# Two graph-attention layers on one core: a planner's costs re-read from the profile, the first adjacency load planned later, one attention ranked last

## The chip, the cores and the metric

The kernel runs on one core of a Trainium2 chip. Its time is the device time of one launch in microseconds; a profile of one further execution shows what each engine did. The engines are PE (TensorE, matmuls; "PEld" is its weight load), DVE (VectorE), ACT (ScalarE), POOL (GpSimd) and SP (SyncE, which only issues DMA transfers here).

## The reference

Input: 32 graphs of 512 nodes with 512 features each (`x`), and an integer adjacency matrix of 512 x 512 per graph (`adj`). Two layers, both of the form x = x + GNN(relu(layernorm(x))):

```python
# layer 0
s_src, s_dst = h @ w_src, h @ w_dst
scores = leaky_relu(s_src[:, :, None] + s_dst[:, None, :] + b, 0.2)
attn = softmax(where(adj + eye == 0, -inf, scores), axis=-1)
x = x + attn @ h
# layer 1: two GAT layers; mask = (adj > 0) | eye
xl = (h @ W1).reshape(B, N, 4, 256)          # W2: one head of 512
e = leaky_relu(asrc[:, :, None, :] + adst[:, None, :, :], 0.2)
attn = softmax(where(mask, e, -1e9), axis=1)
out = einsum('bsdh,bshf->bdhf', attn, xl)    # 4 heads side by side
h = elu(out + b1);  then the same with W2, att2, b2 and one head
x = x + h
```

So each graph has six attentions over 512 x 512: one in layer 0, four heads in the first GAT layer (width 256), and one in the second GAT layer (width 512, called the second attention here).

## The kernel before

All is in float32. Nodes lie in T = 4 tiles of 128 partitions. A graph passes through these pieces, each of which only records operations:

- `load_x`, `load_adj`: x of a graph by SP, its adjacency (converted to bf16) by POOL's queue. `load_adj` runs twice per graph, for layer 0's mask (m0) and for layer 1's (m1).
- `layer0_scores`: `layernorm` (DVE statistics, POOL computes the power -1/2 in L516), `relu_normed` on ACT (L529), two dot products per tile on DVE (L384, in `dot`), the mask `masks0` (DVE L758 and L761; then one DMA transpose m0 -> m0T, L735), and `edge_weights`.
- `edge_weights` builds exp(leaky_relu(a_i + c_j) + mask - m_j). A row of scores comes over all partitions, either by four TensorE transposes (`spread`, L506) or by a DMA through DRAM (`in_lines` L605 and L611, `row_of` L621) and a copy into PSUM on ACT (`in_bank`, L631). DVE takes the masked maximum of each tile (L643, with a small accumulator read after it), sums and leaky-relus the maxima (L649, L651), and the result is brought over all partitions by `spread` (L506) or lines. Then, per tile: Prelu on ACT (L665), subtraction of the maximum on DVE (L668), addition of the mask on POOL (L671), exp on ACT (L674).
- `attend` / `aggregate`: matmuls of E with the values (L684), on DVE a reciprocal of the denominator (L696) and the scaled addition to x (L702). `layer1_head` does the same for a head (L970, L973), then the elu (ACT L987, L990 and DVE L994 or, for the last head, L1009 and L1013), and turns the result round: by two ACT copies and a DMA transpose (L558, L565, L574) or by TensorE (L506, for head 3 only).
- `layer1_project`, `layer2_project`: the products with W1 and W2 in a seven-product (Strassen-like) form, L900, with sums of operands on DVE or POOL (`combine`, L881 or L882), results copied (`taken`: L539 on ACT or L545 on DVE) or added (`added`: L913 on DVE).
- `layer2_out`: the second attention of a graph and the store of its output.

What a graph needs twice is put away in DRAM in between (`spill`, `load_back`).

Nothing runs in the order of the calls. Each call of `op` appends an entry: the engines that may do it, a cost per engine, what it reads and writes, and a shift of its rank. A cost is (time it occupies the engine, time until its result is there). `Plan.run` makes six drafts with different weights of the shifts. Each is a list schedule: the engine that is free first takes the ready operation of lowest rank, buffers are given out as they come free, an operation with two engines goes to the one that comes to it first. The draft with the earliest planned end is built, and each engine then runs its list strictly in order, waiting on semaphores. So a cost changes no instruction as such; it changes the order, the engine of operations that have two, and the buffers.

Costs are given by small functions of the number n of elements per partition: `on_dve(n)` is n/0.96 + 70 ns (85 ns more to its end), `on_act(n, i)` is n/1.2 plus one of three constants (i = 0, 1 or 2: none, one or two per-partition operands), and 60 ns more to its end. The main loop at the end goes over the graphs b: `masks1(b)`, `layer1_project(b)`, `load_back(b - 1)`, `layer2_out(b - 1)`, the four heads of b, `layer0_out(b + 1)`, `layer1_in(b + 1)`, `layer0_scores(b + 2)`, `layer2_project(b)`. For the last graph but one, `layer2_out` is split: its first EARLY tiles come in the loop, the rest after the loop, so with the highest ranks but for the last graph's own.

The planner orders by these lines (rank is the place of the call minus a part of the shift `ahead`; a smaller rank goes first):

```python
draft = self.draft([i - part * ahead for i, ahead in (o[5] for o in self.ops)])
...
_, i = heapq.heappop(now[e])
```

Of the kernel before, what the change touches and what calls it, by code (L numbers as in the profile page):

```python
# [241 lines left out]
def on_dve(n, speed=1.0, scaled_psum=False):  # L242
    one = n / 0.96 / speed + (130.0 if scaled_psum else 70.0)
    return one, one + 85.0


def on_act(n, per_partition=0):

    one = n / 1.2 + (95.0, 140.0, 280.0)[per_partition]
    return one, one + 60.0  # L250


def on_pool(n, narrow=False):
# [15 lines left out]
def kernel(  # L269
# [24 lines left out]
    nc = tc.nc  # L294
    B, N, D = x.shape
    H, F = att_src1.shape
# [17 lines left out]
    def node_tiles(src: bass.AP, b: int) -> bass.AP:  # L314
        return src[b].rearrange("(t p) f -> p t f", p=P)
# [124 lines left out]
    def scores_1(att):  # L440
        for k in range(KD):
            for h in range(H):
                q, kk = QUARTER[k // (KD // 2)][h % 2], k % (KD // 2)
                for i in range(2):
                    op(
                        "DVE", on_dve(F),
                        lambda w=w1_s[q][:, kk, h // 2, :], i=i, h=h: dot(
                            w[:, 2:], flat(att[0])[:, i * HF + h * F : i * HF + (h + 1) * F], w[:, i : i + 1]
                        ),
                        W["w1"]((q, kk)) + att[0](i), W["w1"]((q, kk, h // 2, i)), -LATER, lock=True,  # L450
                    )

    def scores_2(att):
        part = const.tile([P, KH, 2], F32, name="part")
        for k in range(KH):
            (q, r), kk = QUARTER[k // (KH // 2)], k % (KH // 2)
            lo, hi = w2_s[q][:, kk, :], w2_s[r][:, kk, :]
            for i in range(2):
                op(
                    "DVE", on_dve(W2),  # L460
                    lambda lo=lo, i=i, k=k: dot(lo[:, 2:], flat(att[1])[:, i * D : i * D + W2 - 2], part[:, k, i : i + 1]),
                    W["w2"]((q, kk)) + att[1](i), W["w2"](("part", k)), -LATER, lock=True,
                )
                op(
                    "DVE", on_dve(W2),
                    lambda lo=lo, hi=hi, i=i: dot(hi, flat(att[1])[:, i * D + W2 - 2 : (i + 1) * D], lo[:, i : i + 1]),
                    W["w2"]((r, kk)) + att[1](i), W["w2"]((q, kk, i)), -LATER, lock=True,
                )
            op(
                "DVE", on_dve(2), lambda lo=lo, k=k: nc.vector.tensor_add(lo[:, :2], lo[:, :2], part[:, k, :]),  # L470
                W["w2"]((q, kk, 0), (q, kk, 1), ("part", k)), W["w2"]((q, kk, "a")), -LATER,
            )
# [62 lines left out]
    def evict(src, dst, src_of, dst_of, n, bias=None, psum_half=False):  # L535

        def by_act():
            if bias is None:
                nc.scalar.copy(dst_of(), src_of())  # L539
            else:  # L540
                nc.scalar.activation(dst_of(), src_of(), AF.Identity, bias=bias)

        def by_dve():
            if bias is None:
                nc.vector.tensor_copy(dst_of(), src_of())  # L545
            else:
                nc.vector.tensor_scalar(dst_of(), src_of(), -1.0, None, op0=ALU.add)

        op(("ACT", "DVE"), (on_act(n, bias is not None), on_dve(n)), (by_act, by_dve), src, dst)

    def turned(values_of, src, place, results_of, dst):

        e = Buffer("row")
        op(
            "ACT", (1040.0, 1100.0),
            lambda: nc.scalar.copy(  # L558
                e.at.bitcast(U16).rearrange("p (b f) -> p b f", b=2), values_of().bitcast(U16).rearrange("p (f b) -> p b f", b=2)
            ),  # L560
            src + place, e(0),
        )
        op(
            "SP", by_turning(4 * P * N),
            lambda: nc.sync.dma_start(  # L565
                values_of().bitcast(U16).rearrange("p (c n) -> p c n", n=P), e.at.bitcast(U16), transpose=True
            ),
            e(0), src,
        )

        def pair():
            out = results_of()
            k, t = out.shape[1], out.shape[2]
            nc.scalar.copy(  # L574
                out.bitcast(U16).rearrange("p k t (n b) -> p k t n b", b=2),
                values_of().bitcast(U16).rearrange("p (b t k n) -> p k t n b", b=2, k=k, t=t),
            )

        op("ACT", (1160.0, 1220.0), pair, src, dst)

    def spread(part, col_of, ahead):

# [51 lines left out]
    def edge_weights(kind, scores, ac, lines, k, mask_max, mask, near):  # L634


        a_of = lambda t: ac.at[:, k, t : t + 1]
        a_row = spread(scores, a_of, AHEAD) if lines is None else in_bank(row_of(lines, k))
        amax, z, m = Buffer("col"), Buffer("col"), Buffer("col")
        for t in range(T):  # L640
            op(
                "DVE", on_dve(N + 60),
                lambda t=t: nc.vector.tensor_tensor_reduce(  # L643
                    by_blocks(junk), mask_row(mask_max, t), by_blocks(a_row.at), 1.0, LOWEST, ALU.add, ALU.max,
                    accum_out=amax.at[:, t : t + 1],
                ),
                a_row(*ROW) + mask_max(*ROW), amax(t),
            )
        op("DVE", on_dve(T), lambda: nc.vector.tensor_add(z.at, ac.at[:, k + 1, :], amax.at), scores + amax(*ROW), z(0))  # L649
        op(  # L650
            "DVE", on_dve(T), lambda: nc.vector.scalar_tensor_tensor(m.at, z.at, SLOPE, z.at, op0=ALU.mult, op1=ALU.max),  # L651
            z(0), m(0),
        )

        E = Buffer(kind)
        m_row = (
            spread(m(0) + E("place"), lambda t: m.at[:, t : t + 1], AHEAD) if near
            else in_bank(row_of(in_lines(lambda: m.at, m(0), 1), 0))
        )
        c_of = lambda t: ac.at[:, k + 1, t : t + 1]  # L660
        c_row = spread(scores + E("place"), c_of, AHEAD) if lines is None else row_of(lines, k + 1)
        for t in range(T):
            op(
                "ACT", on_act(N, 1),
                lambda t=t: nc.scalar.activation(E.at[:, t, :], c_row.at, AF.Prelu, bias=a_of(t), scale=1.0, alpha=SLOPE),  # L665
                c_row(*ROW) + scores, E(t),
            )
            op("DVE", on_dve(N), lambda t=t: nc.vector.tensor_sub(E.at[:, t, :], E.at[:, t, :], m_row.at), m_row(*ROW) + E(t), E(t))  # L668
            op(
                "POOL", on_pool(N, True),  # L670
                lambda t=t: nc.gpsimd.tensor_add(by_blocks(E.at[:, t, :]), by_blocks(E.at[:, t, :]), mask_row(mask, t)),  # L671
                E(t) + mask(*ROW), E(t), lock=True,
            )
            op("ACT", on_act(N), lambda t=t: nc.scalar.activation(E.at[:, t, :], E.at[:, t, :], AF.Exp), E(t), E(t))  # L674
        return E
# [42 lines left out]
    def load_adj(b, m):  # L718

        first, early = not START.wrote, len(adj_loads) < 3
        adj_loads.append(b)
        op(
            "POOL", (1100.0, 5500.0) if first else (2200.0, 16000.0 if early else 8000.0), lambda: nc.gpsimd.dma_start(m.at, node_tiles(adj, b)),  # L725
            () if first else START(0), m(*ROW) + (START(0) if first else []),
        )

# [57 lines left out]
    def layer0_scores(b):  # L786
        rstd, nmr = layernorm(X[b])
        h0, ac = Buffer("h"), Buffer("ac")
        for t in range(T):
            relu_normed(h0, X[b], t, rstd, nmr)  # L790
            for i, w in ((1, ws_r), (0, wd_r)):
                op(
                    "DVE", on_dve(D), lambda t=t, w=w, i=i: dot(h0.at[:, t, :D], w, ac.at[:, i, t : t + 1]),
                    h0(t) + W["w0"](0, 1), ac((i, t)), lock=True,
                )
        c = ac(*((1, t) for t in ROW))
        op(
            "DVE", on_dve(T), lambda: nc.vector.tensor_scalar(ac.at[:, 1, :], ac.at[:, 1, :], b0_r, None, op0=ALU.add),
            c + W["w0"](2), c,
        )  # L800
        m0, m0T = masks0(b)
        scores = c + ac(*((0, t) for t in ROW))

        L0[b] = (h0, edge_weights("E_one", scores, ac, in_lines(first(ac, 2), scores, 2) if b else None, 0, m0, m0T, not b))
# [266 lines left out]

    EARLY = 1
    load_x(0)
    att = load_constants()
    layer0_scores(0)
# [61 lines left out]
```

## Time and profile before

| | us |
|---|---|
| median of 3 runs | 3646.97 (3645.85 to 3647.93) |
| the profiled execution | 3648.51 |
| its span, first to last instruction | 3646.7 |
| PE busy, matmuls | 3542.6 (97%) |
| DVE busy | 2851.2 (78%) |
| ACT busy | 2264.6 (62%) |
| POOL busy | 1424.6 (39%) |
| mean granted TensorE clock | 0.994 |

The profile's groups name a line, an engine and an operation with its tiles, then count, busy time and mean duration. "Idle before, releaser" is the time its engine stood idle just before, and what ended that. The biggest groups:

```
L684 PE MATMUL acc<-pair,E 128*128 128x257 f32 x4096 | 920.4, 379 | 2.4 <-ACT row L987 2.4
L643 DVE CUSTOM_DVE_ANT_0 junk<-m1T,acc 128x512 bf16<-128x512 bf16 x640 | 436.6, 682 | 11.4 <-PE acc L506 3.4
L674 ACT ACTIVATE E<-E 128x512 f32<-128x512 f32 x512 | 315.6, 623 | 161.7 <-POOL E L671 161.4
L671 POOL TENSOR_TENSOR E<-E,m 128x512 f32<-128x512 f32 x512 | 605.1, 1211 | 455.3 <-DVE E L668 396.7
```

Two records stand for one float32 matmul, and matmuls overlap: the records of one are 0.217 us apart, though each shows 0.38.

### The profile page before, as it was taken

What the parts mean: (1) busy time and instruction counts of PE and PEld (TensorE: products, weight loads), DVE (VectorE), ACT (ScalarE), POOL (GpSimd) and SP (SyncE); (2) the same over time, 40 slices, a digit from 0 to 9 for tenths busy, and PEclk for the clock granted to TensorE, in tenths of its full rate; (3) what the DMA queues carried; (4) which work ended last, traced back from release to release, by engine and by line L of the source; (5) the groups of instructions that cost most, each with busy time, mean ns of one, the idle gap of its engine ahead of it and who ended that gap; (6) DMA issues with size and microseconds to landing.
All of it is one profiled execution on the core that took longest, in us unless ns stands there. A gap on an engine that the chain in (4) does not pass through costs nothing.

```text
span 3646.7 us, 50543 instructions
## 1 busy us (share of the span) xinstructions
PE 3542.6 (97%) x16852; PEld 3036.1 (83%) x16852; DVE 2851.2 (78%) x7367; ACT 2264.6 (62%) x3929; POOL 1424.6 (39%) x1279
## 2 busy tenths in 40 slices
PE   4899999999999999999999999999999999999998
PEld 3788888888888888888888888888888888888887
DVE  7978778877778877778787788877787877887755
ACT  2666566665666665666666667655666656666554
POOL 4534334434334343334343344343343433343422
PEclk9999999999999999999999999999999999999999
DMA  6244433444433444334443334443334443344321
GB/s 172 77 105 119 104 92 104 100 121 113 96 96 103 104 121 112 90 96 105 115 116 98 95 103 99 125 116 86 97 110 105 119 108 89 103 103 118 105 73 41
DMA packets 510374, 378.82 MB, mean 104 GB/s; under 512 B 348344, under 2 KB 386976, under 8 KB 510112
## 3 DMA queue, kind: packets, MB, share of 16 engines
q1 hardware_dynamic: 476320, 342.03, 32.8%
q0 software_dynamic: 33792, 33.56, 6.1%
q8 instruction: 132, 2.16, 0.2%
q14 instruction: 130, 1.06, 0.1%
HBM read 257.16 MB, written 68.01 MB: 89 GB/s over the span
## 4 chain that ended last, share of the span: by engine, by line
PE 80%; DVE 14%; ACT 2%; issue 1%; DMA 1%; POOL 0%; DVEq 0%; ACTq 0%; SPq 0%
PE acc L684 45%; PE acc L900 32%; DVE junk L384 5%; PE acc L506 3%; DVE v L1013 1%; DVE hT L881 1%; DVE hT L545 1%; DVE col L521 1%; DVE col L649 1%; ACT h L529 1%; DVE v L973 1%; PE acc L605 1%; DVE junk L643 1%; DVE E L881 1%; DVE xl L913 1%
## 5 line engine op out<-in xcount | busy, mean ns | idle before, releaser
L684 PE MATMUL acc<-pair,E 128*128 128x257 f32 x4096 | 920.4, 379 | 2.4 <-ACT row L987 2.4
L684 PEld LDWEIGHTS acc<-pair,E 128*128 128x128 f32 x4096 | 771.7, 189 | 115.5 <-ACT row L987 2.8
L671 POOL TENSOR_TENSOR E<-E,m 128x512 f32<-128x512 f32 x512 | 605.1, 1211 | 455.3 <-DVE E L668 396.7
L900 PE MATMUL acc<-w_T,E 128*128 128x257 f32 (+1 forms) x2048 | 517.9, 380 | 0.8 <-POOL w_T L488 0.8
L684 PE MATMUL acc<-h,E_one 128*128 128x256 f32 (+1 forms) x2048 | 491.2, 381 | 8.6 <-ACT E_one L674 7.5
L684 PE MATMUL acc<-xl,E_one 128*128 128x257 f32 x1984 | 447.9, 381 | 2.7 <-ACT E_one L674 2.7
L643 DVE CUSTOM_DVE_ANT_0 junk<-m1T,acc 128x512 bf16<-128x512 bf16 x640 | 436.6, 682 | 11.4 <-PE acc L506 3.4
L900 PEld LDWEIGHTS acc<-w_T,E 128*128 128x128 f32 x2048 | 385.4, 189 | 61.0 <-POOL w_T L488 1.5
L684 PEld LDWEIGHTS acc<-h,E_one 128*128 128x128 f32 x2048 | 380.8, 191 | 63.6 <-ACT E_one L674 8.3
L684 PEld LDWEIGHTS acc<-xl,E_one 128*128 128x128 f32 x1984 | 371.8, 190 | 54.7 <-ACT E_one L674 3.1
L674 ACT ACTIVATE E<-E 128x512 f32<-128x512 f32 x512 | 315.6, 623 | 161.7 <-POOL E L671 161.4
L913 DVE TENSOR_TENSOR pair<-acc,pair 128x258 f32<-128x258 f32 (+1 forms) x390 | 165.4, 426 | 293.7 <-PE acc L900 219.2
L539 ACT COPY pair<-acc 128x258 f32<-128x258 f32 (+1 forms) x456 | 165.8, 370 | 320.5 <-PE acc L900 315.8
L665 ACT ACTIVATE E<-row,ac 128x512 f32<-128x512 f32 x512 | 341.1, 707 | 2.4 <-DMA row<-lines 2.4
L668 DVE TENSOR_TENSOR E<-E,acc 128x512 f32<-128x512 f32 x512 | 330.4, 678 | 6.5 <-PE acc L506 3.1
L671 POOL TENSOR_TENSOR E_one<-E_one,m0T 128x512 f32<-128x512 f32 x128 | 144.4, 1152 | 355.6 <-DVE E_one L668 355.6
L725 POOL DMA_DIRECT2D m<-in_adj_dram x64 | 51.5, 805 | 590.8 <-DVE col L643 540.7
L900 PE MATMUL acc<-w,hT 128*128 128x258 f32 x1024 | 265.5, 384 | 0.6 <-issue 0.5
L900 PE MATMUL acc<-w,E 128*128 128x257 f32 (+1 forms) x1024 | 264.2, 380 | 0.0
L702 DVE SCALAR_TENSOR_TENSOR x<-acc,r,x 128x256 f32<-128x256 f32 x512 | 239.7, 479 | 30.9 <-PE acc L684 22.8
L529 ACT ACTIVATE h<-x,col,col 128x512 f32<-128x512 f32 x256 | 187.6, 804 | 109.0 <-DVE col L521 109.0
L539 ACT COPY xl<-acc 128x257 f32<-128x257 f32 x218 | 77.6, 369 | 284.9 <-PE acc L900 284.8
(113 smaller groups left out, 6171.9 us busy)
## 6 DMA issues: line engine op xcount, KB each, us to landing
row<-lines SPq DMA_DIRECT2D x442, 256.0 KB, 3.4
x<-in_x_dram SPq DMA_DIRECT2D x32, 1024.0 KB
m<-in_adj_dram POOLq DMA_DIRECT2D x64, 512.0 KB, 6.3
spill<-x SPq DMA_DIRECT2D x32, 1024.0 KB, 4.2
x<-spill SPq DMA_DIRECT2D x32, 1024.0 KB
out_dram<-x SPq DMA_DIRECT2D x30, 1024.0 KB, 4.2
v<-row SPq DMA_TRANSPOSE x192, 2.7
out_dram<-x SPq DMA_DIRECT2D x8, 256.0 KB, 2.0
```

What stands on the lines that cost most here:

```text
L384: nc.vector.scalar_tensor_tensor(junk[:, : vector.shape[1]], values, 1.0, vector, op0=ALU.mult, op1=ALU.mult, accum_out=out)
L529: lambda: nc.scalar.activation(h.at[:, t, :D], X.at[:, t, :], AF.Relu, bias=nmr.at[:, t : t + 1], scale=rstd.at[:, t : t + 1]),
L539: nc.scalar.copy(dst_of(), src_of())
L643: lambda t=t: nc.vector.tensor_tensor_reduce(by_blocks(junk), mask_row(mask_max, t), by_blocks(a_row.at), 1.0, LOWEST, ALU.add, ALU.max, a ...
L665: lambda t=t: nc.scalar.activation(E.at[:, t, :], c_row.at, AF.Prelu, bias=a_of(t), scale=1.0, alpha=SLOPE),
L668: op("DVE", on_dve(N), lambda t=t: nc.vector.tensor_sub(E.at[:, t, :], E.at[:, t, :], m_row.at), m_row(*ROW) + E(t), E(t))
L671: lambda t=t: nc.gpsimd.tensor_add(by_blocks(E.at[:, t, :]), by_blocks(E.at[:, t, :]), mask_row(mask, t)),
L674: op("ACT", on_act(N), lambda t=t: nc.scalar.activation(E.at[:, t, :], E.at[:, t, :], AF.Exp), E(t), E(t))
L684: lambda s=s: nc.tensor.matmul(acc.at[:, :n], E.at[:, s, node_block(t)], of(s), start=(s == 0), stop=(s == T - 1)),
L702: lambda acc=acc, r=r, f=f, t=t: nc.vector.scalar_tensor_tensor(X.at[:, t, f], acc.at[:, :HD], r.at, X.at[:, t, f], op0=ALU.mult, op1=ALU. ...
L900: lambda k=k: nc.tensor.matmul(acc.at[:, :width], at[a]()[:, k, node_block(r)], weight_of(w, k, c), start=(first and k == 0), stop=(k == n ...
L913: op("DVE", on_dve(width), lambda: nc.vector.tensor_add(place(), acc.at[:, :width], place()), acc(0) + token, token)
```

## The change

Most lines change the planner's costs. Only one thing is different in what the calls record: EARLY is 0, so all four tiles of graph 30's second attention are recorded after the loop.

```diff
 def on_act(n, per_partition=0):
-    one = n / 1.2 + (95.0, 140.0, 280.0)[per_partition]
-    return one, one + 60.0
+    one = n / 1.2 + (95.0, 186.0, 280.0)[per_partition]
+    return one, one + 130.0
+
+def on_act_copied(n):
+    one = n / 1.2 + 52.0
+    return one, one + 160.0
...
# scores_1: dot products with the attention vectors of the first GAT layer
-                        "DVE", on_dve(F),
+                        "DVE", on_dve(F + 125),
...
# scores_2, twice
-                    "DVE", on_dve(W2),
+                    "DVE", on_dve(W2 + 125),
...
# evict
-        op(("ACT", "DVE"), (on_act(n, bias is not None), on_dve(n)), (by_act, by_dve), src, dst)
+        op(("ACT", "DVE"), (on_act_copied(n) if bias is None else on_act(n), on_dve(n)), (by_act, by_dve), src, dst)
...
# turned
-            "ACT", (1040.0, 1100.0),
+            "ACT", (945.0, 1100.0),
...
-        op("ACT", (1160.0, 1220.0), pair, src, dst)
+        op("ACT", (1062.0, 1220.0), pair, src, dst)
...
# edge_weights, the masked maximum
-                "DVE", on_dve(N + 60),
+                "DVE", on_dve(N + 10),
...
# load_adj
-            "POOL", (1100.0, 5500.0) if first else (2200.0, 16000.0 if early else 8000.0), ...
+            "POOL", (1100.0, 11000.0) if first else (2200.0, 16000.0 if early else 8000.0), ...
...
# layer0_scores
-                    "DVE", on_dve(D), lambda t=t, w=w, i=i: dot(...),
+                    "DVE", on_dve(D + 125), lambda t=t, w=w, i=i: dot(...),
...
-    EARLY = 1
+    EARLY = 0
```

More of the change, by code (lines that the diff above doesn't have):

```diff
@@ L464, in scores_2 @@
                 op(
-                    "DVE", on_dve(W2),
+                    "DVE", on_dve(W2 + 125),
                     lambda lo=lo, hi=hi, i=i: dot(hi, flat(att[1])[:, i * D + W2 - 2 : (i + 1) * D], lo[:, i : i + 1]),
@@ L724, in load_adj @@
         op(
-            "POOL", (1100.0, 5500.0) if first else (2200.0, 16000.0 if early else 8000.0), lambda: nc.gpsimd.dma_start(m.at, node_tiles(adj, b)),
+            "POOL", (1100.0, 11000.0) if first else (2200.0, 16000.0 if early else 8000.0), lambda: nc.gpsimd.dma_start(m.at, node_tiles(adj, b)),
             () if first else START(0), m(*ROW) + (START(0) if first else []),
@@ L792, in layer0_scores @@
                 op(
-                    "DVE", on_dve(D), lambda t=t, w=w, i=i: dot(h0.at[:, t, :D], w, ac.at[:, i, t : t + 1]),
+                    "DVE", on_dve(D + 125), lambda t=t, w=w, i=i: dot(h0.at[:, t, :D], w, ac.at[:, i, t : t + 1]),
                     h0(t) + W["w0"](0, 1), ac((i, t)), lock=True,
```

## The prediction, made before the changed kernel was run

> **What bounds the kernel now.** I read the windows view first, for how much TensorE idles and where.
>
> ```profile
> core 0: us, PE busy (x) PEld busy (x) DVE busy (x) ACT busy (x) POOL busy (x), PEclk, DMA share, GB/s
> 0.00:100.00 100.00, 51.54 (x203) 40.30 (x203) 79.02 (x241) 25.94 (x48) 46.01 (x44) 0.91 0.64 168
> 100.00:200.00 100.00, 89.93 (x405) 74.76 (x406) 84.68 (x221) 61.02 (x102) 43.79 (x38) 0.95 0.25 71
> 200.00:2000.00 1800.00, 1784.14 (x8540) 1532.91 (x8539) 1426.32 (x3674) 1150.63 (x2005) 709.79 (x638) 1.00 0.40 106
> 3500.00:3647.00 147.00, 130.40 (x585) 110.08 (x583) 73.12 (x180) 64.64 (x116) 36.06 (x31) 0.94 0.22 63
> ```
>
> The first 200 us hold 58.5 us of TensorE idle (48.46 + 10.07), the last 147 hold 16.6, and the middle 15.9 in 1800. The chain of waits repeats every 110.81 us in the middle, one period per graph, so the middle loses about 1 us per graph. No matmul is added or dropped by this change, so only these gaps can move. The wait view, cut to 1000 to 3216 us (20 periods), says what the middle gaps are:
>
> ```profile
> PE acc L506 <- DVE col L651: 11.7, 20, 0.7
> PE acc L506 <- DVE v L1013: 4.8, 20, 0.2
> ```
>
> Per period that is 0.58 us for one broadcast of a head's row maximum (L506 after DVE's L651), and 0.24 us for one transpose of head 3's result. Around the first of them DVE has no gap:
>
> ```profile
> 2003.39 0.16 DVE L651 SCALAR_TENSOR_TENSOR col<-col 128x4 f32<-128x4 f32 x1
> 2003.51 0.69 DVE L643 CUSTOM_DVE_ANT_0 junk<-m1T,acc 128x512 bf16<-128x512 bf16 x1
> ...
> 2009.46 1.06 DVE L649 TENSOR_TENSOR col<-ac,col 128x4 f32<-128x4 f32 x1
> 2010.45 0.68 DVE L643 CUSTOM_DVE_ANT_0 junk<-m1T,acc 128x512 bf16<-128x512 bf16 x1
> ...
> 2011.45 0.14 DVE L651 SCALAR_TENSOR_TENSOR col<-col 128x4 f32<-128x4 f32 x1
> ```
>
> The reader is to see a stretch where DVE, not TensorE, paces the work: between two maxima 8.06 us pass on DVE (2003.39 to 2011.45), while TensorE has 7.1 us of work between the two broadcasts. The start is a chain of its own; TensorE's timeline:
>
> ```profile
> 33.59 15.88 PE L684 MATMUL acc<-h,E_one 128*128 128x257 f32 x64 [3.42 <-ACT E_one L674]
> 55.51 3.68 PE L506 MATMUL acc<-ident,h 128*128 128x128 f32 x16 [6.04 <-ACT h L529]
> 73.17 0.38 PE L605 MATMUL acc<-ident,ac 128*8 128x128 f32 x1 [9.30 <-DVE ac L798]
> ```
>
> **What the Trainium skill says.** "GPSIMD Engine Reference", Specifications, gives GpSimd an SBUF interface shared with VectorE, with contention for DVE instructions with two SBUF inputs. The trace agrees: the L649 above, four elements wide with both inputs in SBUF, took 1.06 us where the same operation took 0.15 at 2002.71, and it ended with one of POOL's four 1.13 us mask additions (2006.00 to 2010.50). The planner knows nothing of this for L649. "DMA: Bandwidth & Descriptors", Queues, rings and completion order, says that each DMA engine takes its ring's descriptors in order. The first mask's transpose (DMA into m0T) fits it: eight weight loads were still outstanding at its issue, and it landed 9.9 us later.
>
> **The change part by part.** The edits alter planned costs only; so I compare the changed program's order of instructions with the trace.
>
> *Costs.* Some come nearer to the trace: four Prelus (L665) take 2.56 us, 0.62 apart (planned 0.567, now 0.613), two copies of 258 columns stand 0.26 apart (planned 0.310, now 0.267), the interleaving copies 0.95 and 1.06. One goes away from it: four masked maxima (L643) with their accumulator reads take 2.80 us (2101.23 to 2104.03); the plan had 4 x 0.666 = 2.66 and now has 2.46. So in the DVE-paced stretch the new plan is 0.34 us per head too hopeful, before 0.14. Over the program 88 evictions of 258 columns move from ACT to DVE (three per graph, 0.34 us each), 52 additions of 512 columns from DVE to POOL, 27 of 2x256 back. These lie in the projections, where DVE waits for TensorE anyway (gaps of 0.4 to 4 us in that timeline), so I price them at nothing; with that cover gone they would be about 1 us per graph.
>
> *The middle.* TensorE's order repeats every 286 matmuls in both programs. A matmul pair of records is 0.435 us. I go broadcast by broadcast.
> - First: a copy of the last projection result now stands on DVE ahead of the second attention's subtractions. TensorE finishes that product 0.43 us later than before, at 2099.5 of this trace's time; then come 0.2 latency, 0.34 + 0.2 copies, 2.4 subtractions, 2.8 maxima, 0.7 small ones: L651 at 2106.15, broadcast possible at 2106.35. TensorE is there at 2105.26 + 2 x 0.435 = 2106.13. Stall 0.2, before none.
> - Second: DVE gets one more L702 (0.40), TensorE one more matmul (0.435). No stall.
> - Third: TensorE has 13 matmuls since the second broadcast, before 15: 6.2 us. DVE drops one L970 and one L973 (0.5 us) and keeps the rest: 8.06 - 0.5 = 7.57, if L649 again runs into POOL's additions, which start 0.76 us after the first subtraction in both. The spare 0.39 us that before had at the second broadcast is gone. Stall 7.57 - 6.2 = 1.37, before 0.58. With no port wait it would be 0.5.
> - Fourth: 18 matmuls in place of 20 (8.35 us with the broadcast); DVE has one L994 and one L973 fewer, one mask conversion more: 8.9 - 0.5 = 8.4. Stall 0.1.
> - Head 3's transpose: nine matmuls stand ahead of it in place of six, 1.3 us more than needed. Its 0.24 goes.
> Sum 0.2 + 0 + 1.37 + 0.1 = 1.7 against 0.82: +0.87 us per graph. The order repeats for 28 graphs: +24 us. Bounds: every such stall gone, -0.82 x 28 = -23; all port waits at their longest (1.1 us at two more places), half the time, +1.9 x 28 = +53. I take +24, because each term is a count of rows with a duration, and the same count gives before's 0.58 back (8.06 + 0.2 - 7.1 - 0.6 of slack).
>
> *The start.* The mask is expected later (11 us, before 5.5), so SP's queue now holds the transpose into m0T behind all of the second layer's weights and graph 1's x, nine loads further down. These are 3.7 MB; DMA is busy to 45 us in the trace at some 270 GB/s. The second mask load of that pile is issued later, so the pile ends at 42 to 43. m0T then lands there, not at 27.3. And POOL's queue has graph 1's rstd (L516), which needs that x and DVE's four statistics (3.1 us), ahead of the first four mask additions: these begin at about 46 in place of 31.73. Queued behind them is everything: ACT's exps, the first attention, DVE's x. So the first attention starts near 48 and the first product near 73, where before had 59.2. What is won back: after 16 records of products before's TensorE waited 9.30 us for graph 1's scores (L798), and lesser stalls of 2.1 followed; the new order has 26 matmuls ahead of that transpose, 11 us, and the scores are ready. All 112 product records take 24.4 us, so they end near 99; the first head then waits for its rows, to about 109, where before began it at 114.3 but had done half of graph 1's attention (7 us) too. Sum +2 us. Earlier things (ACT's first h at 10.8, before 16.36) gain nothing, since the mask gates. Bounds: m0T early after all, -8; nothing won back, +14.
>
> *The end.* EARLY = 0 ranks graph 30's whole second attention last. Yet TensorE takes whatever is ready: in the new order its 32 matmuls again all stand before graph 31's last projection (3, 7, 11 and 11 among the heads; before 4, 8, 11, 7 and 2). None is left for the waits of 3.00 and 2.74 us before the last attention. The two that stood between the last two head transposes are gone, where before still waited 1.18: +0.5, bounds -1 and +2.
>
> Sum: span 3646.7 + 24 + 2 + 0.5 = 3673. The profiled execution took 3648.5, 1.8 above its span and 1.5 above the median of the runs; so 3673.5, and I say 3673.
>
> **The rivals.**
> - *Paced as before.* The port waits fall elsewhere, DVE's spare time absorbs its copies, and the start is even: within 7 us. For it: the two orders differ by two or three matmuls per stretch only. Against: DVE has no gap there. About 3648.
> - *The better costs win (faster).* ACT's latency, planned at 60 ns before and 130 now, was what made the broadcasts late, and the 9.3 us at the start come without the late mask: 3647 - 23 - 9 = 3615. For it: nearly all edits are nearer to the trace. Against: in 20 periods ACT caused TensorE only two waits, 1.9 us.
> - *The late mask alone (slower).* The middle stays, the start loses its 14 us because later work has the same chain to wait for: 3661. It decides once m0T lands after 40.
> - *EARLY does not do what it says*: held by the order itself, and part of my forecast.
>
> **How the numbers follow.** Forecast 0.55, of which nearly all is slower; paced as before 0.18; faster 0.15; late mask alone 0.12. A change under 0.2% (7.3 us) can't be told from none here. Faster: 0.15. Same: 0.18 less its tails plus 0.02 of the forecast's low end, 0.17. Slower: 0.68. The forecast's own range is 3655 to 3695; the range for 8 in 10 goes down to 3640 to hold the paced-as-before case.
>
> **What would show it.** In the middle: the period above 111.3 us, DVE's L651 as releaser of TensorE's L506 with 1.2 to 2 us per graph in place of 0.58, and no wait on L1013. At the start: m0T landing after 40, the first attention at 46 to 50, no 9 us wait on L798. At the end: 64 records of xl,E_one before the last projection. A period of 110.8 or less refutes the middle step; a first attention before 38 refutes the step on the mask.

## The result, and the profile after

| | before | after |
|---|---|---|
| median, 20 runs each | 3646.84 us (3645.11 to 3650.36) | 3653.77 us (3650.93 to 3661.58) |
| the profiled execution | 3648.51 | 3652.49 |
| its span | 3646.7 | 3650.7 |

The ratio is 1.0018, 95% interval 1.0012 to 1.0025: 0.18% slower, 6.9 us. It lies just inside the 0.2% that I had called no change, and 19 us under the forecast. The profiled executions are only 4.0 us apart: before's was 1.7 above its median, after's 1.3 below.

The windows view of the changed kernel, the same stretches as shown of before (busy us of each engine with its count, the granted clock, DMA):

```profile
0.00:100.00 100.00, 48.13 (x202) 39.45 (x202) 80.17 (x228) 25.57 (x47) 38.74 (x39) 0.97 0.58 161
100.00:200.00 100.00, 86.22 (x387) 70.84 (x388) 86.26 (x223) 59.54 (x99) 45.80 (x40) 0.91 0.30 74
200.00:2000.00 1800.00, 1784.54 (x8526) 1527.50 (x8525) 1406.98 (x3700) 1139.35 (x1954) 731.35 (x648) 1.00 0.41 105
3500.00:3647.00 147.00, 133.56 (x614) 112.30 (x613) 75.86 (x184) 68.79 (x122) 40.98 (x35) 0.97 0.21 62
```

TensorE does 7.1 us less in the first 200 us (3.4 + 3.7), and the same in the middle: 1784.5 against 1784.1. The wait view of 1000 to 3216 us says why the middle is even:

```profile
PE acc L511 <- DVE col L656: 15.2, 20, 0.8
PE acc L689 <- ACT E_one L679: 2.6, 3, 1.6
```

(L511, L654, L656 of the changed kernel are L506, L649, L651 of before: lines past 253 stand five further down.) TensorE spreads a row of maxima over the partitions four times per graph. The third of these broadcasts waits 0.76 us per graph in place of 0.58; the 0.24 before head 3's transposes are gone. 0.76 against 0.82: nothing.

To split the span I follow one record that comes twice per graph, TensorE's transposition of four maxima into a line (L605 before, L610 after). The third of its 62 is at 204.3 us before and 208.7 after, the 61st at 3420.4 and 3425.3. So the start gives +4.4 us, the 29 periods between +0.5, and the end -0.9 (226.3 and 225.4 us to the last instruction). Most periods are 110.82 before and 110.74 after; the others are longer, by 5 us in all after and by 2 before, which takes back what the common period gains. TensorE's timeline of the start:

```profile
46.30 15.91 PE L689 MATMUL acc<-h,E_one 128*128 128x257 f32 x64 [13.02 <-ACT E_one L679]
72.68 6.48 PE L905 MATMUL acc<-w,hT 128*128 128x258 f32 x26
101.66 2.09 PE L905 MATMUL acc<-w_-T,hT 128*128 128x258 f32 x4 [3.83 <-DVE pair L918]
109.37 1.11 PE L511 MATMUL acc<-ident,col 128*128 128x128 f32 x4 [3.22 <-DVE col L656]
113.23 2.08 PE L689 MATMUL acc<-pair,E 128*128 128x257 f32 x4 [2.75 <-ACT E L679]
```

The first attention starts 12.7 us later than before (33.59), the first product 13.5 later; after that the 9.3 us wait for graph 1's scores is gone, and the three waits shown from 101.66 on, together 9.8 us, and one of 1.8 us at L610 stand ahead of the first head. What the first mask additions waited for is seen on GpSimd:

```profile
43.26 1.20 POOL L521 TENSOR_TENSOR col<-col,minus_half 128x4 f32<-128x4 f32 x1 [5.70 <-DVE col L519]
44.44 3.56 POOL L676 TENSOR_TENSOR E_one<-E_one,m0T 128x512 f32<-128x512 f32 x3
```

By the DMA's semaphore the mask m0T had landed at 39.7 us, just behind graph 1's x at 37.9. The additions then stood 4.7 us longer in GpSimd's queue, behind L521, which waited for VectorE's statistics of that x.

### The profile page after: what moved, and what is told of

It reads as the page before. It is cut to its first block, busy times and chain, and to the rows that moved or that the text cites. A ratio compares the mean times of both kernels' runs of the same rounds, so it can differ in the third digit from the quotient of the medians.

```text
span 3650.7 us, 50258 instructions
## 1 busy us (share of the span) xinstructions
PE 3542.4 (97%) x16852; PEld 3027.7 (83%) x16852; DVE 2827.3 (77%) x7427; ACT 2249.2 (62%) x3844; POOL 1471.7 (40%) x1304
## 4 chain that ended last, share of the span: by engine, by line
PE 75%; DVE 20%; issue 1%; DMA 1%; ACT 0%; POOL 0%; SPq 0%; DVEq 0%; ACTq 0%
PE acc L905 41%; PE acc L689 30%; DVE junk L648 7%; DVE E L673 4%; DVE x L707 4%; PE acc L511 4%; DVE E_one L673 2%; DVE col L654 1%; PE acc L610 0%; DVE r L701 0%; DVE v L978 0%; DVE pair L550 0%; DVE col L656 0%; DMA lines<-row 0%; DMA row<-lines 0%
## 5 line engine op out<-in xcount | busy, mean ns | idle before, releaser
L676 POOL TENSOR_TENSOR E<-E,m 128x512 f32<-128x512 f32 x512 | 594.5, 1192 | 408.2 <-DVE E L673 272.0
L689 PE MATMUL acc<-h,E_one 128*128 128x257 f32 (+1 forms) x2048 | 479.9, 380 | 16.7 <-ACT E_one L679 15.7
L648 DVE CUSTOM_DVE_ANT_0 junk<-m1T,acc 128x512 bf16<-128x512 bf16 x640 | 436.0, 681 | 13.8 <-PE acc L511 3.4
L544 ACT COPY pair<-acc 128x258 f32<-128x258 f32 (+1 forms) x368 | 137.9, 375 | 304.0 <-PE acc L905 299.6
L730 POOL DMA_DIRECT2D m<-in_adj_dram x64 | 51.6, 806 | 577.1 <-DVE col L648 527.6
L676 POOL TENSOR_TENSOR E_one<-E_one,m0T 128x512 f32<-128x512 f32 x128 | 144.7, 1154 | 331.6 <-DVE E_one L673 331.6
L905 PE MATMUL acc<-w,E 128*128 128x257 f32 (+1 forms) x1024 | 271.8, 380 | 0.0
L707 DVE SCALAR_TENSOR_TENSOR x<-acc,r,x 128x256 f32<-128x256 f32 x512 | 238.8, 477 | 28.3 <-PE acc L689 26.0
L905 PE MATMUL acc<-w,pair 128*128 128x257 f32 x1024 | 253.5, 380 | 0.0
```

The source lines that it names most:

```text
L648: lambda t=t: nc.vector.tensor_tensor_reduce(by_blocks(junk), mask_row(mask_max, t), by_blocks(a_row.at), 1.0, LOWEST, ALU.add, ALU.max, a ...
L689: lambda s=s: nc.tensor.matmul(acc.at[:, :n], E.at[:, s, node_block(t)], of(s), start=(s == 0), stop=(s == T - 1)),
L707: lambda acc=acc, r=r, f=f, t=t: nc.vector.scalar_tensor_tensor(X.at[:, t, f], acc.at[:, :HD], r.at, X.at[:, t, f], op0=ALU.mult, op1=ALU. ...
L905: lambda k=k: nc.tensor.matmul(acc.at[:, :width], at[a]()[:, k, node_block(r)], weight_of(w, k, c), start=(first and k == 0), stop=(k == n ...
```

## The experiments

Medians of 4 to 21 runs; the kernel before, beside them, had 3646.7 to 3648.6, so a difference of 2 us between two rows of the table says nothing. "Period" is the commonest distance of the marker above in one profiled execution, "start" its third record.

| run | edits on before, or the kernel it starts from | us | start | period |
|---|---|---|---|---|
| changed kernel | all | 3653.77 | 208.7 | 110.74 |
| e1 | changed, first mask at 5.5 us | 3653.76 | 203.7 | 110.74 |
| e2 | changed, EARLY = 1 | 3653.15 | 208.2 | 110.75 |
| e3 | changed, maxima at N + 60 | 3643.12 | 217.5 | 110.29 |
| e16 | changed without these three edits | 3636.61 | 207.4 | 110.29 |
| e6 | changed, attention really kept | 3660.50 | 207.7 | 110.76 |
| e5 | changed, half of L707 | 3645.03 | 208.8 | 110.47 |
| e9 | changed, L654 planned at 950 | 3635.45 | 213.8 | 110.13 |
| e10 | changed, maxima at N + 92 | 3661.46 | 204.6 | 110.5 to 113.5 |
| e13 | changed, L654 from PSUM | 3653.09 | 210.2 | 110.75 |
| e17 | changed, L654 and L656 from PSUM | 3629.81 | 209.4 | 109.91 |
| e4 | on_act_copied alone | 3624.65 | 205.1 | 110.02 |
| e7 | e4, half the attention kept | 3627.36 | 205.9 | 110.02 |
| e8 | on_act_copied, on_act | 3631.37 | 204.7 | 110.08 |
| e11 | on_act_copied, L654 at 950 | 3648.11 | 207.7 | 110.75 |
| e12 | on_act_copied, turned | 3616.10 | 202.5 | 109.75 |
| e14 | e12, L654 from PSUM | 3619.42 | 206.6 | 109.75 |
| e15 | e12, first mask at 11 us | 3615.86 | 203.6 | 109.75 |
| e18 | e15, L654 and L656 from PSUM | 3615.21 | 203.9 | 109.75 |

### Which edit moved the time: e1, e2, e3, e16

```diff
# e1                          # each starts from the changed kernel
-   (1100.0, 11000.0) if first
+   (1100.0, 5500.0) if first
# e2
-    EARLY = 0
+    EARLY = 1
# e3
-   "DVE", on_dve(N + 10),
+   "DVE", on_dve(N + 60),
# e16: all three
```

> The changed kernel with the first adjacency load planned at 5.5 us again. All engines run the same order as the changed kernel from about the fourth graph on; only the start differs. Theory A (the start pays for the late mask): the changed kernel is 4.4 us behind at the end of its first graph, its middle takes the same as before and its end 0.9 less; so with m0T landing near 27 and the first attention near 34, nearly all of the difference goes: about 3648 to 3650, 4 to 6 us less than the changed kernel. Theory B (my forecast's start, the late mask costs only about 2 because later waits are won back): 2 us less, about 3652. Theory C (the difference is in the middle): no change, 3653 to 3654. Period 110.74 in all three.

> The changed kernel with EARLY = 1 again. Start and middle have the same order on every engine; only the last 280 of 9173 TensorE instructions differ: three matmuls of graph 30's second attention stand between the last two head transposes, none in the changed kernel. My forecast's end term: 0.5 us less than the changed kernel (range 2 less to 1 more). Rival: the whole attention does fill waits at the end, and undoing it costs 3 us or more.

> The changed kernel with the masked maximum planned at N + 60 again (0.666 us; the trace shows 0.70 for each). In the repeating part TensorE then has 15 matmuls between the second and third broadcast of row maxima, 13 in the changed kernel, and VectorE nearly the same rows in that stretch (8.8 against 8.7 us by the mean durations). Theory A (the cost that went away from the trace makes the third broadcast late): its wait of 0.77 us per graph falls by up to 0.8, the period from 110.74 to 110.0 to 110.2, 15 to 20 us in 28 graphs: about 3635. Theory B (the lateness only moves to another broadcast or transpose): period 110.7 to 110.9, within 3 us of the changed kernel.

> The changed kernel without three of its edits: maxima at N + 60, first mask at 5.5, EARLY = 1. What is left are the costs that come nearer to the trace. Its repeating part has the matmul counts of the run with the maxima at N + 60 (period 110.28, a wait of 0.47 for the first weights of layer 0). Theory A: period 110.28 and a start near 205 in place of 217, so about 3631. Theory B (its start is the one with late first graphs): 3640 to 3645.

e1: theory A had the start right (203.7, five us earlier) and the time wrong: no gain came of it (3653.76 and 3653.77). With the early mask the order of the first graphs is another one, and the four periods after the third record take 111.6, 111.5, 112.0 and 111.9 us: 4.1 us more than four of 110.74. So the five us are given back at once. Even its start has a longer wait for graph 1's scores than before:

```profile
PE acc L610 <- DVE ac L803: 13.0, 1, 13.0
```

e2: 0.6 us under the changed kernel, with ranges that overlap: EARLY as such does nothing that can be told. e3: the lowered maxima cost 10.6 us. The third broadcast's wait is gone, but only half of it is gained, since the next one in line comes up, the first weights of layer 0's attention, 0.47 us per graph:

```profile
PE acc L689 <- ACT E_one L679: 9.5, 20, 0.5
```

e16 has that period too, and a start ten us earlier than e3's; the A expectations of the two were 8 and 6 us too low. The two edits that e16 takes back beyond e3's, mask and EARLY, are worth 6.5 us here, though each alone gave nothing on the changed kernel (e1, e2): what an edit is worth depends on the order that the others make. The costs that came nearer to the trace make the kernel 0.3% faster (ratio 0.9968, 0.9955 to 0.9980); the other three edits take that away and more.

### The attention really kept for the end: e6, e7

```diff
# the matmuls of graph 30's kept tiles also wait for the last projection result of graph 31
-                E(s) + values(*part(s)) + result("place"), acc(0),
+                E(s) + values(*part(s)) + result("place") + list(after), acc(0),
...
-    layer2_out(B - 2, ROW[EARLY:], False)
+    layer2_out(B - 2, ROW[EARLY:], False, L2[B - 1][1]((1, T - 1)))
# e6 on the changed kernel; e7 on e4, with EARLY = 2
```

> The changed kernel, with graph 30's second attention really kept: its matmuls also wait for the last graph's last projection result. Only the last 220 TensorE instructions differ: all 32 matmuls (13.9 us) stand behind the last projection, none between the last graph's heads. Theory A (they are worth what they fill): the waits of 0.7, 3.0 and 2.8 us before the last attention go, but 13.9 us of work stand there, and the heads they left become VectorE's; 2 to 6 us slower than the changed kernel. Theory B (the end was short of work, the heads not): 4 to 6 us faster.

> The kernel of the copies alone (3624.65), with the last two tiles of graph 30's second attention kept behind the last projection (EARLY = 2 and the same wait). Only the end differs. 16 matmuls, 6.9 us, against waits of 6.4 us there, and 6.9 us less work among the last graph's heads. Theory A: 1 to 4 us faster, about 3622. Theory B (the heads then wait for VectorE as long as they ran before): even or slower, 3625 to 3630.

6.7 and 2.7 us slower than the kernels they start from (e7's runs overlap with e4's at the edge). In e6's wait view from 3500 us on, the waits before the last attention are gone and larger ones stand among the heads:

```profile
PE acc L511 <- DVE col L656: 9.3, 2, 4.9
PE acc L511 <- DVE v L1018: 3.9, 2, 2.4
PE acc L689 <- ACT E L679: 2.8, 1, 2.8
```

13.9 us of matmuls found only some 6.5 us of waits to fill; where they had stood, VectorE's maxima are late. All of e6's loss lies there: from the 61st record to the last instruction it takes 232.1 us, the changed kernel 225.4. So the edit gains nothing where it does nothing (the changed kernel, where all 32 matmuls ran ahead of the last projection), and loses where it does what its words say.

### What the third broadcast waits for: e5, e9, e10, e13, e17

The changed kernel's VectorE, from the second broadcast's row (L656 at 2122.22) to the third's:

```profile
2122.22 0.15 DVE L656 SCALAR_TENSOR_TENSOR col<-col 128x4 f32<-128x4 f32 x1
...
2127.59 0.16 DVE L975 RECIPROCAL r<-acc 128x1 f32<-128x1 f32 x1
2127.67 0.92 DVE L654 TENSOR_TENSOR col<-ac,col 128x4 f32<-128x4 f32 x1
2128.51 0.67 DVE L648 CUSTOM_DVE_ANT_0 junk<-m1T,acc 128x512 bf16<-128x512 bf16 x1
2129.11 0.08 DVE L648 DVE_READ_ACCUMULATOR2_ANT col<- 128x1 f32 x1
2129.11 0.47 DVE L978 SCALAR_TENSOR_TENSOR v<-acc,r,b_r 128x256 f32<-128x256 f32 x1
2129.51 0.19 DVE L656 SCALAR_TENSOR_TENSOR col<-col 128x4 f32<-128x4 f32 x1
```

and GpSimd beside it, four additions in a row, 1.12 us each:

```profile
2125.18 4.50 POOL L676 TENSOR_TENSOR E<-E,m 128x512 f32<-128x512 f32 x4 [5.92 <-DVE E L673]
```

The four-element sum L654 ends at 2128.59, when the third addition does (2125.18 + 3 x 1.12). The leaky maximum L656, 0.19 us, ends at 2129.70, with the fourth (2125.18 + 4.50 = 2129.68).

```diff
# e5: the second attention's update of x, half its columns
-  X.at[:, t, f], acc.at[:, :HD], r.at, X.at[:, t, f], op0=ALU.mult, op1=ALU.add
+  X.at[:, t, f][:, :m], acc.at[:, :m], r.at, X.at[:, t, f][:, :m], op0=ALU.mult, op1=ALU.add   # m = HD // 2
# e9: planned cost of L654
-  op("DVE", on_dve(T), lambda: nc.vector.tensor_add(z.at, ac.at[:, k + 1, :], amax.at), scores + amax(*ROW), z(0))
+  op("DVE", (950.0, 1020.0), lambda: nc.vector.tensor_add(z.at, ac.at[:, k + 1, :], amax.at), scores + amax(*ROW), z(0))
# e10
-  "DVE", on_dve(N + 10),
+  "DVE", on_dve(N + 92),
# e13 (first pair), e17 (both)
-  tensor_add(z.at, ac.at[:, k + 1, :], amax.at), scores + amax(*ROW), z(0)
+  tensor_add(z.at, a_row.at[:, :T], amax.at), a_row(0) + amax(*ROW), z(0)
-  scalar_tensor_tensor(m.at, z.at, SLOPE, z.at, op0=ALU.mult, op1=ALU.max), z(0), m(0)
+  scalar_tensor_tensor(m.at, z.at, SLOPE, a_row.at[:, :T], op0=ALU.mult, op1=ALU.max), a_row(0) + z(0), m(0)
```

> The changed kernel, where the second attention's scaled addition to x (L707) covers 128 of its 256 columns; the other half of x gets no second attention. The order is that of the changed kernel on every engine. Theory A (the third broadcast waits for VectorE, whose rows run without a gap from its last projection copy to the third maximum, 23.3 us): eleven L707 stand in that run, each about 0.13 us shorter, 1.5 us in all, more than the wait of 0.77; the wait goes, the period falls to about 110.0, the time to about 3632. Theory B (something else than VectorE's rows paces it: GpSimd's additions or a buffer): the period stays at 110.7, the time at 3653.

> The changed kernel, with one more planned cost read from the trace: the four-element sum L654 at 950 ns (planned 74; it took 920 before the third broadcast). In the repeating part TensorE then has 24 matmuls between the second and third broadcast, in place of 13. Theory A (the third broadcast is late because the plan does not know this row and what stands behind the reciprocal L975): the wait of 0.77 goes, period 109.8 to 110.1, 20 to 26 us less than the changed kernel, 3628 to 3634. Theory B (the wait moves): period above 110.5, above 3645.

> The changed kernel with the masked maximum planned as the trace has it (N + 92, 0.70 us; N + 10 gives 0.61). TensorE has 18 matmuls between the second and third broadcast, in place of 13. Theory A (this cost alone decides the third broadcast's wait): period 109.9 to 110.3, 3632 to 3643, no slower than with N + 60 (3643.1). Theory B (a nearer cost means nothing, only the order that comes out): period anywhere from 109.8 to 110.8, the start as in the changed kernel or 9 us later as with N + 60.

> The changed kernel, where the sum L654 takes the row of scores in PSUM in place of the column in SBUF as its second operand. It shifts only the exponent that the division takes out again. The repeating part has the order of the changed kernel. Theory A (the wait at the third broadcast is L654's 0.92 us beside GpSimd's additions): L654 there takes about 0.15, the wait of 0.77 goes, the period falls to about 110.0, time about 3632. Theory B (the reciprocal before it or the maxima after it are as late without it): the period stays above 110.5.

> The changed kernel, with both small rows, the sum L654 and the leaky maximum L656, taking the row of scores in PSUM as their second operand; both shift only the exponent. The repeating part has the matmul counts of the changed kernel. Theory A (the first row with two SBUF operands behind GpSimd's additions waits for them, whichever it is): both take about 0.15, the broadcast is ready 0.8 us earlier, the wait of 0.77 goes, period 109.9 to 110.1, 3630 to 3635. Theory B (the row after these, or TensorE's own product, is as late): period above 110.5.

e5 falls between its theories: the period loses 0.27, not 0.77. (Of the eleven updates in that run three are layer 0's and kept their width; the other eight still are 1.0 us.) Its VectorE shows what is left:

```profile
2124.08 0.17 DVE L975 RECIPROCAL r<-acc 128x1 f32<-128x1 f32 x1 [0.17 <-PE acc L689]
2124.16 0.92 DVE L654 TENSOR_TENSOR col<-ac,col 128x4 f32<-128x4 f32 x1
```

VectorE now reaches the reciprocal early and waits for TensorE's own product; the sum behind it in the queue takes its 0.92 us as ever, up to 2125.08, the end of the third addition (2121.67 + 3 x 1.12 = 2125.03). The additions begin 2.13 us after the second broadcast, in the changed kernel 2.42 (2122.76 to 2125.18): these 0.29 us are what the period gained.

e13 takes the sum's second SBUF operand away. That sum is short now, but the row below is held in its place:

```profile
2127.73 0.14 DVE L654 TENSOR_TENSOR col<-acc,col 128x4 f32<-128x4 f32 x1
...
2128.79 0.97 DVE L656 SCALAR_TENSOR_TENSOR col<-col 128x4 f32<-128x4 f32 x1
```

L656 reads the same SBUF column twice, and ends at 2129.76, with GpSimd's fourth addition (2125.24 + 4.50). The wait of TensorE stays at 15.2 us in 20 periods. e17 gives L656 a PSUM operand as well:

```profile
2113.28 0.14 DVE L654 TENSOR_TENSOR col<-acc,col 128x4 f32<-128x4 f32 x1
...
2114.34 0.15 DVE L656 SCALAR_TENSOR_TENSOR col<-col,acc 128x4 f32<-128x4 f32 x1
```

No wait on L656 is left in its 20 periods; the time falls by 24.0 us to 3629.81, as theory A had it. A different order is no rival here: in the graph shown, the changed kernel, e5, e13 and e17 have the same instructions in the same order on TensorE, VectorE, ScalarE and GpSimd. This settles the wait: a VectorE row with two SBUF operands that comes while an addition runs is held to that addition's end. It is what the Trainium skill states in "SBUF — State Buffer", SBUF: two separate sides (of a VectorE instruction with two SBUF inputs and a GpSimd instruction that reads SBUF, the one that starts first keeps the other out until it is done); the 0.92, 0.97 and 0.14 us agree. e13 and e17 are probes: in them the softmax is no longer shifted by its row's maximum, which a kernel for scores of any size would need.

e9 tells the planner of the 0.92: the broadcast's wait goes, 18 us are gained (theory A: 20 to 26), and 0.53 us per graph come up at layer 0's first weights. e10 gives the maxima the cost that the trace shows and is the slowest of these: 26.5 us of waits in 20 periods at layer 0's first weights again. Theory A there falls, and the periods go beyond B's range too; a planned cost that is right is no better for it than a wrong one.

### The other costs, and the fastest version: e4, e8, e11, e12, e14, e15, e18

```diff
# before, with one to three of the change's edits
# e4   on_act_copied        e8   on_act_copied, on_act        e12  on_act_copied, turned
# e15  e12 and the first mask at 11000
# e11  e4 and the edit of e9   e14  e12 and the edit of e13   e18  e15 and the edits of e17
```

> The kernel before with one edit alone, the planned cost of ScalarE's copies (on_act_copied). Its start has the order of before for the first 280 TensorE instructions. In the repeating part TensorE has 19 matmuls between the second and third broadcast, before 15 (1.74 us more work), and VectorE 1.7 us more rows there. Theory A (the stretch's wait is VectorE's rows less TensorE's work, counted from the second broadcast): the wait stays at 0.5 to 0.6 us, period 110.8, time within 3 us of before. Theory B (more matmuls in that stretch take the wait away): period near 110.2, 15 us faster than before.

> The kernel before with two edits: ScalarE's costs and latency (on_act 186 and 130) and its copies. In the repeating part TensorE has 14 matmuls between the second and third broadcast, where the copies alone gave 19; head 3's transposes have 8 in front as in the changed kernel. Theory A (the latency edit takes the gain of the copies away): third broadcast waits about 0.6 us, nothing before head 3's transposes, period 110.5 to 110.7, 3640 to 3648. Theory B (another edit does it): period near 110.0, 3624 to 3630.

> The kernel before with the copies' cost and L654 planned at 950 ns. 21 matmuls between the second and third broadcast, 19 between first and second (before 15 and 21). Theory A: no wait at the third broadcast, the period 109.75 to 110.05, with the start of the copies alone: 3617 to 3626. Theory B (another wait of about 0.3 to 0.5 per graph comes up): 3627 to 3640.

> The kernel before with the copies' cost and that of the two interleaving copies (945, 1062). 19 matmuls before the third broadcast as with the copies alone, nine before head 3's transposes in place of six. With the copies alone the only steady wait is 0.26 us per graph on L803. Theory A (that wait stays, the rest is the same): period 110.0, 3622 to 3627. Theory B (it goes with the moved copies): period 109.75, 3615 to 3620.

> The kernel of the copies and turns (3616.1), with the same sum from PSUM, in the same repeating order. There L654 took 0.15 before the third broadcast, and no broadcast is waited for. Theory A of the run before: no change, within 2 us, period 109.75. Theory B (such sums cost elsewhere too): 3 to 10 us faster.

> The kernel of the copies and turns with the first adjacency load planned at 11 us. The repeating part has the same order, only the first graphs differ. Theory A (the late mask costs the start some 4 to 5 us, as the changed kernel's first graph shows against the one with 5.5): 3619 to 3622. Theory B (it gives back what it costs within the first graphs): 3615 to 3617. Theory C (the wait of 9.2 us for graph 1's scores goes and nothing comes for it): 3608.

> The kernel of the copies and turns with the late mask (3615.86), with both rows from PSUM and the same order on every engine. In its repeating part both rows took 0.15 already. Theory A: within 2 us of 3615.9. Theory B (reading PSUM there costs TensorE or ACT): slower by more than 2.

e4 is 22.5 us faster than before, by one cost; its theory A fell. Its VectorE run, without a gap from 2086.26 to the third broadcast's row at 2109.97, is as long as before's (23.7 and 23.5 us), but TensorE has 24.6 us of work in that time where before had 23.1; and L654 falls outside the additions (0.15 us). Which of the two took the wait away was not separated. e8 refutes its theory A: on_act adds 6.7 us, most of the gain stays. e11 refutes its A: the third broadcast is free, but the period is 110.75, by 1.27 us at layer 0's first weights, more than its B allowed. That chain passes four engines; e11's timeline:

```profile
2094.26 0.60 ACT L636 COPY acc<-row 128x512 f32<-128x512 f32 x1
...
2096.07 2.47 DVE L673 TENSOR_TENSOR E_one<-E_one,acc 128x512 f32<-128x512 f32 x4
...
2096.84 2.27 POOL L676 TENSOR_TENSOR E_one<-E_one,m0T 128x512 f32<-128x512 f32 x2 [12.20 <-DVE E_one L673]
2098.02 0.63 ACT L679 ACTIVATE E_one<-E_one 128x512 f32<-128x512 f32 x1 [3.16 <-POOL E_one L676]
...
2098.70 0.48 PE L689 MATMUL acc<-h,E_one 128*128 128x257 f32 x1 [1.27 <-ACT E_one L679]
```

e12 has neither wait, only 0.39 us per graph on the scores L803, and a period of 109.75: B's number, not B's reason, for that wait was to go and was 0.26 in e4. Why the period is shorter all the same, the wait view doesn't show. e14 and e18 have PSUM operands where no row was held, and in the repeating part nothing changes; e14 lost 4 us in its start. e15 against e12 shows no cost of the late mask as a whole here either (3615.86 and 3616.10): it takes the wait of 9.2 us for graph 1's scores away and puts others in its place. e18 has the lowest median, 3615.21 us, ratio to before 0.9906 (0.9892 to 0.9919), but its runs overlap with e15's, which keeps the softmax's maximum. Two of the change's costs and its mask are in both; the change as a whole is some 38 us slower.

## Why the prediction was wrong

Of 26 us of forecast the middle step's 24 failed. The direction came out right, but not by the step that it rested on: the middle gave +0.5 us in the profiled execution, the start +4.4.

- **Third broadcast, "Stall 7.57 - 6.2 = 1.37"**: the term that was mis-sized. It measured 0.76. Two parts: "The spare 0.39 us that before had at the second broadcast is gone" was wrong, for VectorE's row began at 2122.22 and TensorE came to its broadcast at 2122.76, so that of these 0.54 us, less the 0.2 of latency, 0.34 were still spare; and VectorE's stretch took 7.29 us (2122.22 to 2129.51), not 7.57. 1.37 - 0.34 - 0.28 = 0.75. First and fourth broadcast, put at 0.2 and 0.1, have no wait in the wait view. So 28 times 0.87 became 28 times -0.06, and the period of 110.74 lies under the 110.8 that was to refute the step.
- **The way of counting** was the deeper fault. I summed rows from one broadcast to the next and took the reserve at each end from a guess. e5 shows that the sum of rows isn't what decides; e13 and e17 show the wait that does, to the end of GpSimd's additions. The prediction had it ("if L649 again runs into POOL's additions"), as a row's length in a sum: 0.5 would be left without it. None is left.
- **Head 3's transposes**: their wait is gone, as said (with eight matmuls ahead, not nine).
- **The maxima's cost, "goes away from the trace"**: its sign was right, 10.6 us (e3). The reason wasn't: e10, with the true value, is slower than either.
- **Evictions "at nothing"**: no such copy turned up on TensorE's waits, but the planned cost of these copies alone moves 22.5 us (e4), through the order and the choice of engine. That an edit of a cost works through every place of the order had no term in my sum.
- **The start**: the times were right, additions from 44.4 (said 46), attention 46.3 (48), product 72.7 (73), but not that "the mask gates": m0T landed at 39.7, not at 42 to 43, and the last thing waited for was graph 1's rstd ahead of the additions in GpSimd's queue, which the text had too. (Seven weight loads, not eight, were outstanding at the transpose's issue in the kernel before, by their semaphores; they and the mask landed in the order of issue. And 29 matmuls, not 26, stood ahead of the scores' transpose.) What comes after was put 4 us too early: the first head at 113.2, not 109, by the waits shown above. +4.4 for +2. That undoing it gains nothing in two orders (e1, e15) I hadn't seen: the mask's time changes the order of the first graphs, and they give it back.
- **The end**: +0.5 said, -0.9 in the profiled execution, nothing to tell in e2.
- **The rivals**: "paced as before" came nearest in size, within 7 us, but only in part by its reasons: the orders differ by two or three matmuls, as it said, yet the port wait stayed at the third broadcast, and the start wasn't even. My argument against it, that VectorE has no gap there, says that VectorE is behind, not by how much. "The better costs win" is true of e16, but not through ACT's latency: e8, which adds it together with another cost of ScalarE, is slower than e4.

What is open: the medians differ by 2.9 us more than the profiled executions, and after's runs scatter more widely. One trace shows a way: ACT waits for a line from DRAM, and an exp that TensorE needs stands behind that copy in ACT's queue:

```profile
1550.68 0.59 ACT L636 COPY acc<-row 128x512 f32<-128x512 f32 x1 [2.06 <-DMA row<-lines]
1551.21 0.62 ACT L679 ACTIVATE E_one<-E_one 128x512 f32<-128x512 f32 x1
```

TensorE lost 1.60 us there. Whether this makes the scatter wasn't tried. Nor was it tried why the orders of the first graphs differ in cost by up to 15 us (202.5 to 217.5).

## What to carry to other kernels

Where a scheduler orders the work, an edit of one planned cost is judged by the waits of the order that comes out, since costs nearer to the trace gave anything from 22 us less to 8 us more here; look for a wait that repeats in every period, and follow it to a single row. A tiny row that takes many times its usual time beside another engine's work is such a place: other operands freed it with the order unchanged (e17), while another cost takes the wait away only if the order that comes out happens to do so (e4 was 22.5 us faster for it, e9 18 us, and e10 made a longer wait elsewhere). And work that is to be kept for a gap needs a dependency that keeps it, and must be missed nowhere else.

## What the runs showed of the hardware

- A four-element VectorE row with two SBUF operands took 0.92 to 1.06 us beside GpSimd's additions, where the lines above show it, and 0.15 otherwise; with one operand in PSUM it took 0.14 at the same place. The same column read twice counts as two operands (L656, 0.97 us in e13).
- The hold ends with the addition, whatever is left of it: over the whole trace of the changed kernel, all 64 rows L654 and L656 that began more than 0.1 us before the end of a GpSimd addition (L676) ended 0.02 us after it, and took 0.18 to 1.08 us. In e17, with one operand in PSUM, 63 such rows took 0.13 to 0.16. A row of 512 elements with two SBUF operands (the elu's L999) ended 0.55 us after the addition, all 37 of them: its work seems to begin only then.
- Not every GpSimd instruction holds: 57 rows L656 that began while GpSimd issued a DMA (L730) took 0.15 us. And rows with one tensor in PSUM and one in SBUF kept their 0.67 and 0.47 us beside the additions (L648, L978); the per-partition scalar r that L978 also takes from SBUF made no difference.
- I hadn't expected the hold to move to the next such row at its full length: freeing one row gained nothing (e13), freeing both gained 24.0 us (e17).
